# A graph network on one core: the node matrix as one float32r product of 258 columns, with every part of the step in a new order

## The chip, the cores and the metric

The kernel runs on one core of a Trainium2 chip. The metric is the device time of one execution in microseconds (us). The engines are named as in the profile: PE (TensorE, with PEld for its weight loads), DVE (VectorE), ACT (ScalarE), POOL (GpSimd) and SP (SyncE, which issues most transfers here).

## The reference

There are 128 graphs of 128 nodes with 512 features. Each goes through two layers. Cut to what matters:

```python
h = maximum(layernorm(x), 0)
# layer 0
H  = (adj != 0)                       # 128 x 128 of zeros and ones
w  = adj[0, :]                        # first row, a weight for each column
Dn = 1 / (H @ w)                      # per node
Be = 1 / H.sum(axis=0)                # per column
S(v) = Dn * (H @ (Be * (H.T @ v)))
r = layer_norm(relu(S(h @ W1.T) + b1), gamma, beta)     # 1024 wide
x = x + (S(r @ W2.T) + b2 + h)
# layer 1
h = maximum(layernorm(x), 0)
agg = adj @ h / maximum(adj.sum(axis=1), 1e-6)
x = x + relu(concat(h, agg) @ W.T)
```

`H @ diag(Be) @ H.T` is a symmetric 128 x 128 matrix. The kernel calls it the node matrix and computes it once for each graph; `H @ w` is one more column of the same product.

## The kernel before

One graph is worked on as a whole: its 128 nodes lie on the 128 partitions. The large weights stay in SBUF. Each of them, and each activation that meets one, is kept as three float32r parts: high `h`, low `l` and a rest `d`. A product with a weight (`product`) is eight or sixteen 512-column matmuls into one PSUM bank (high with high, low with low) and four or eight with the rests into a second bank. Products are named by their PSUM tiles: `rm`/`rd` for W1 (two halves, with `w10` and `w11`), `gm`/`gd` for W2, `bm`/`bd` and `am`/`ad` for the two halves of W.

Two products are in plain float32, which PE runs as two passes: `conv1_nodes` (`pz`, the node matrix on h, four matmuls of 128 columns) and `node_matrix` (`ps_s`, the node matrix itself, 128 columns and one for `H @ w`).

The program is a software pipeline. `head` starts the first graphs and splits the weights, `step(s)` runs once for s = 3 to 124, and `tail` ends. In a step several graphs are in work: s + 2 (its incidence matrix), s + 1 (node matrix and `conv1_nodes`), s and s - 1 (layer 0), s - 2, s - 3 and s - 4 (layer 1). The calls in `head`, `step` and `tail` are written out by hand, and every engine runs its instructions in exactly that order. Nothing reorders them.

What the change and the prediction touch:

- `load_adjb` brings adj in blocks of 32 x 32. `incidence` transposes it on DVE (L385), scales the column of weights (L387), makes zeros and ones and counts them (L389), bounds the count (L391) and inverts it (L392). `incidence_scale` multiplies by the inverse. `node_matrix` (L404) is the product, and ACT copies it to `s` (L406).
- `node_scale` makes `Dn` from the last column with four small DVE instructions (L415 to L418).
- `conv1_high`, `conv1_low`, `conv1_rest` split `pz` into `z` (ACT L460, DVE L464 and L467). `conv1_weights` multiplies it with W1. `conv1_main` (ACT L509) and `conv1_out` (DVE L514) bring the result back, and `conv1_bias` adds b1 on POOL (L81).
- `inner_sums`, `inner_spread`, `scales`, `shifts`, `inner_norm` are the layer norm. `inner_out` and `inner_in` send its result through DRAM to transpose blocks, `inner_turn` (DVE L550) turns within blocks, and `inner_high`, `inner_low`, `inner_rest` split it.
- `conv2_weights` multiplies with W2, `conv2_weights_out` (DVE L653) brings it back, `conv2_bias` adds on POOL, `conv2_high`, `conv2_low`, `conv2_rest`, `node_high`, `node_rest` (L682, L683) split both sides, and `conv2_nodes` (L701 to L703) multiplies; `conv2_out` (L713) adds the result to x.
- `layer1_*` and `mean_*` are layer 1. `mean_operator` sums adj (L339), bounds and inverts the sum (L340, L341), `mean_scale` scales adj, `mean_out` and `mean_in` send it through DRAM, `aggregate` multiplies, `finish` (L803) adds to x.
- `residual` adds h to x on POOL and then b2: for graphs 3 to 120 by a transfer on POOL's queue that accumulates into x (`moved`, L91), for the other ten by POOL additions.
- `combine` (L81) is the helper of all plain additions and subtractions; on POOL it works in pieces of 256 columns. `scaled` (L301 on ACT, L303 elsewhere) is the helper of all products with a column. `fill` puts products without use ahead of others.

PSUM has six banks for large products and two that `ps_s`, `pz` and `py` share.

Of the kernel before, what the change touches and what calls it, by code (L numbers as in the profile page):

```python
# [7 lines left out]
FP = mybir.dt.float32  # L8
# [8 lines left out]
EPS_DEG = 1e-6  # L17
# [7 lines left out]
def gnn_kernel(  # L25
# [61 lines left out]
    def steady(g):  # L87
        return FIRST <= g <= LAST
# [71 lines left out]
    b2_bc = const.tile([P, D], FP, name="b2_bc")  # L160
    c0 = const.tile([P, D], FP, name="c0")
    gb = const.tile([P, 2, KH], FP, name="gb")
# [169 lines left out]
    SB, HT, S, DN, H0, Z, PZ, SPLIT = ({} for _ in range(8))  # L332

    @stage
    def mean_operator(g):

        a = ADJ.pop(g)
        deg = small.tile([P, 1], FP, tag="deg", name="deg", bufs=2)
        nc.vector.tensor_reduce(deg, a, AX.X, ADD)  # L339
        nc.vector.tensor_scalar(deg, deg, EPS_DEG, 1.0 / 4096.0, MAX, MUL)  # L340
        nc.vector.reciprocal(deg, deg)  # L341
        ADJ[g] = a, deg
# [37 lines left out]
    @stage  # L380
    def incidence(g):


        HT[g] = at = pool.tile([P, P], FP, tag="ht", name="adjt")
        nc.vector.transpose(at, ADJB.pop(g))  # L385
        SB[g] = sb = small.tile([P, P + 1], FP, tag="sb", name="sb")
        nc.vector.tensor_scalar(sb[:, P : P + 1], at[:, 0:1], DOWN_12, None, MUL)  # L387
        cnt = small.tile([P, 1], FP, tag="cnt", name="cnt", bufs=2)
        nc.vector.tensor_scalar(at, at, 0.0, None, ALU.not_equal, ADD, accum_out=cnt)  # L389

        nc.vector.tensor_scalar(cnt, cnt, 1.0, None, MAX)  # L391
        nc.vector.reciprocal(cnt, cnt)  # L392
        SB[g] = sb, cnt

    @stage
    def incidence_scale(g, eng):
        SB[g], cnt = SB[g]
        scaled(eng, SB[g][:, :P], HT[g], cnt)


    @stage
    def node_matrix(g):
        ps = small_bank("ps_s")
        nc.tensor.matmul(ps[:, : P + 1], HT.pop(g), SB.pop(g), start=True, stop=True)  # L404
        s = small.tile([P, P + 1], FP, tag="s", name="s", bufs=4)
        copy(s, ps[:, : P + 1], AF.Copy, scale=4096.0 if steady(g) else 1.0)  # L406
        S[g] = s[:, :P]
        DN[g] = s[:, P : P + 1]

    @stage  # L410
    def node_scale(g):
        w = DN[g]
        DN[g] = dn = small.tile([P, 4], FP, tag="dinv", name="dinv", bufs=6)
        inv = dn[:, 2:3]
        nc.vector.tensor_scalar(inv, w, TINY, None, MAX)  # L415
        nc.vector.reciprocal(inv, inv)
        nc.vector.scalar_tensor_tensor(dn[:, 0:1], w, 0.0, inv, ALU.is_gt, MUL)
        nc.vector.tensor_scalar(dn[:, 1:2], dn[:, 0:1], ONE_UP, None, MUL)  # L418
        if not steady(g):
            nc.vector.tensor_scalar(dn[:, 3:4], dn[:, 0:1], DOWN_12, None, MUL)  # L420
# [14 lines left out]
    @stage  # L435
    def residual(g, eng=nc.gpsimd):
        combine(eng, X[g], X[g], H0[g], ADD)
        if steady(g):
            moved(X[g], b2_bc)
        else:  # L440
            combine(eng, X[g], X[g], b2_bc, ADD)
# [373 lines left out]
    def step(s):  # L815
        node_high(s - 2)
        layer1_high(s - 3)
        conv2_bias(s - 2)
        inner_out(s - 1)
        inner_in(s - 1)  # L820
        conv2_high(s - 2)
        node_rest(s - 2)
        node_matrix(s + 1)
        mean_out(s - 3)
        layer1_low(s - 3, nc.vector)
        layer1_self_main(s - 4)
        conv1_weights(s, 1)
        mean_in(s - 3)
        conv2_low(s - 2, nc.vector)
        layer1_self_out(s - 4)  # L830
        conv2_rest(s - 2)
        conv2_nodes(s - 2)
        finish(s - 4)
        load_adj(s - 2)
        layer1_rest(s - 3)
        x_norm(s + 1)
        conv1_main(s, 0)
        conv2_out(s - 2)
        store(s - 4)
        conv1_nodes(s + 1)  # L840
        conv1_main(s, 1)
        conv1_out(s, 1)
        conv1_out(s, 0)
        conv1_high(s + 1)
        conv1_bias(s, 1)
        layer1_mean(s - 3)
        inner_turn(s - 1)
        layer1_sums(s - 2)
        conv1_bias(s, 0)
        conv1_low(s + 1)  # L850
        layer1_self(s - 3)
        layer1_mean_main(s - 3)
        layer1_spread(s - 2)
        load_adjb(s + 3)
        inner_high(s - 1)
        scales(s - 2, 3)
        mean_transpose(s - 3)
        shifts(s - 2, 3, nc.gpsimd)
        layer1_norm(s - 2)
        inner_sums(s)  # L860
        layer1_mean_out(s - 3)
        layer1_mean_high(s - 3)
        inner_low(s - 1, nc.vector)
        mean_rest(s - 3)
        inner_rest(s - 1)
        layer1_mean_low(s - 3, nc.vector)
        layer1_mean_rest(s - 3)
        inner_spread(s)
        scales(s, 2)
        shifts(s, 2, nc.gpsimd)  # L870
        conv2_weights(s - 1)
        layer1_trip_out(s - 2)
        residual(s + 1)
        incidence(s + 2)
        inner_norm(s)
        aggregate(s - 3)
        node_scale(s + 1)
        load_x(s + 2)
        mean_operator(s - 2)
        conv2_main(s - 1)  # L880
        layer1_trip_in(s - 2)
        conv2_weights_out(s - 1)
        x_sums(s + 2)
        x_spread(s + 2)
        mean_scale(s - 2, nc.scalar)
        conv1_rest(s + 1)
        layer1_turn(s - 2)
        incidence_scale(s + 2, nc.gpsimd)
        conv1_weights(s + 1, 0)
        scales(s + 2, 1)  # L890
        shifts(s + 2, 1, nc.vector)

    def head():
        load_w1(0, 0)
        load_x(0)
        load_adjb(0, nc.scalar)
        copy(eps_root, eps, AF.Sqrt)
        w1[0].high(0)
        w1[0].low(0)
        incidence(0)  # L900
        load_x(1)
        x_sums(0)
        x_sums(1, "A")
        fill(128)
        x_spread(0)
        load_w1(0, 1)
        w1[0].high(1)
        scales(0, 1)
        shifts(0, 1, nc.scalar)
        unit()  # L910
        load_adjb(1)
        incidence_scale(0, nc.vector)
        w1[0].low(1)
        x_norm(0)
        node_matrix(0)
        load_w1(1, 0)
        incidence(1)
        w1[0].rest(0, nc.vector)
        load_w1(1, 1)
        load_w2(0)  # L920
        incidence_scale(1, nc.scalar)
        w1[0].rest(1, nc.vector)
        conv1_nodes(0)
        load_affine()
        load_x(2)
        conv1_high(0)
        x_spread(1)
        conv1_low(0)
        w1[1].high(0)
        fill(128)  # L930
        conv1_rest(0)
        w1[1].high(1)
        load_bias(b2_bc, b2)
        load_bias(b1_bc, b1)
        scales(1, 1)
        node_matrix(1)
        residual(0)
        w1[1].low(0)
        shifts(1, 1, nc.scalar)
        conv1_weights(0, 0)  # L940
        x_norm(1)
        conv1_nodes(1)
        w1[1].low(1)
        load_w2(1)
        beta_row(0)
        beta_row(1)
        w1[1].rest(0, nc.vector)
        conv1_high(1, True)
        scale_w2(1, nc.gpsimd)
        w1[1].rest(1, nc.vector)  # L950
        x_sums(2)
        scale_w2(0, nc.scalar)
        beta_row(2)
        x_spread(2)
        beta_row(3)
        node_scale(0)
        conv1_low(1)
        scales(2, 1)
        scale_w2(2, nc.gpsimd)
        conv1_main(0, 0)  # L960
        scale_w2(3, nc.scalar)
        conv1_weights(0, 1)
        shifts(2, 1, nc.scalar)
        w2[0].high(0)
        conv1_main(0, 1)
        conv1_out(0, 0)
        w2[0].high(1)
        conv1_rest(1)
        conv1_out(0, 1)
        conv1_bias(0, 1, nc.vector)  # L970
        x_norm(2)
        conv1_weights(1, 0)
        load_adjb(2)
        w2[0].low(1)
        incidence(2)
        conv1_bias(0, 0)
        incidence_scale(2, nc.vector)
        beta_row(4)
        inner_sums(0)
        inner_spread(0)  # L980
        beta_row(5)
        beta_row(6)
        residual(2)
        scales(0, 2)
        scale_w2(4, nc.scalar)
        node_scale(1)
        shifts(0, 2, nc.scalar)
        load_adjb(3)
        beta_row(7)
        residual(1)  # L990
        scale_w2(7, nc.vector)
        inner_norm(0)
        beta_out()
        load_w3(1)
        node_matrix(2)
        w2[0].low(0)
        conv1_nodes(2)
        incidence(3)
        scale_w2(5, nc.scalar)
        scale_w2(6, nc.gpsimd)  # L1000
        w2[1].high(0)
        w2[0].rest(1)
        inner_out(0)
        conv1_high(2)
        w2[1].low(0)
        w2[0].rest(0)
        load_x(3)
        conv1_low(2)
        conv1_weights(1, 1)
        conv1_main(1, 0)  # L1010
        incidence_scale(3, nc.scalar)
        conv1_out(1, 0)
        conv1_main(1, 1)
        w2[1].high(1)
        inner_in(0)
        node_matrix(3)
        conv1_rest(2)
        conv1_bias(1, 0)
        conv1_out(1, 1)
        load_w3(0)  # L1020
# [423 lines left out]
```

## Time and profile before

| | us |
|---|---|
| median of 3 runs (2457.92 to 2458.43) | 2458.43 |
| profiled execution | 2458.89 |
| its span | 2457.1 |
| one step of the loop, between two starts of L404 | 18.86 |
| PE busy | 2437.2 |
| DVE busy | 2340.8 |
| ACT busy | 2061.8 |
| POOL busy | 1016.1 |

The span runs from the first to the last profiled instruction, and the time of the execution contains it. Busy times of instructions on one engine overlap a little, since the next may start before the last element of the one before is out. For PE, the distance between two starts is the surer measure.

### The profile page before, as it was taken

What the parts mean: (1) busy time and instruction counts of PE and PEld (TensorE: products, weight loads), DVE (VectorE), ACT (ScalarE), POOL (GpSimd) and SP (SyncE); (2) the same over time, 40 slices, a digit from 0 to 9 for tenths busy, and PEclk for the clock granted to TensorE, in tenths of its full rate; (3) what the DMA queues carried; (4) which work ended last, traced back from release to release, by engine and by line L of the source; (5) the groups of instructions that cost most, each with busy time, mean ns of one, the idle gap of its engine ahead of it and who ended that gap; (6) DMA issues with size and microseconds to landing.
All of it is one profiled execution on the core that took longest, in us unless ns stands there. A gap on an engine that the chain in (4) does not pass through costs nothing.

```text
span 2457.1 us, 41143 instructions
## 1 busy us (share of the span) xinstructions
PE 2437.2 (99%) x11300; PEld 2023.8 (82%) x11300; DVE 2340.8 (95%) x5358; ACT 2061.8 (84%) x4494; POOL 1016.1 (41%) x1560
## 2 busy tenths in 40 slices
PE   8999999999999999999999999999999999999998
PEld 6788888888888888888888888888888888888886
DVE  8899999999999999999999999999999999999987
ACT  8888888888888888888888888888888888888885
POOL 5434343444344434443444434343434343434452
PEclk9999999999999999999999999999999999999999
DMA  7454554445444544454455444544554454445432
GB/s 193 132 139 136 141 143 139 136 142 146 136 137 140 149 135 138 139 150 132 139 144 145 136 138 142 143 136 138 144 141 137 138 146 139 136 138 145 127 121 94
DMA packets 425943, 342.30 MB, mean 139 GB/s; under 512 B 178544, under 2 KB 341872, under 8 KB 425712
## 3 DMA queue, kind: packets, MB, share of 16 engines
q1 hardware_dynamic: 407888, 308.66, 41.0%
q0 software_dynamic: 17248, 30.95, 7.2%
q8 instruction: 89, 1.46, 0.3%
q14 instruction: 142, 1.16, 0.2%
q10 hardware_dynamic: 576, 0.07, 0.0%
HBM read 166.21 MB, written 142.34 MB: 126 GB/s over the span
## 4 chain that ended last, share of the span: by engine, by line
PE 83%; DVE 12%; issue 2%; ACT 2%; DMA 1%; SPq 0%; POOL 0%; DVEq 0%; ACTq 0%; POOLq 0%
PE gm L489 16%; PE rm L489 16%; PE bm L489 8%; PE am L489 8%; PE gd L494 8%; PE rd L494 8%; PE bd L494 4%; PE ad L494 4%; PE pz L447 4%; PE am L791 2%; PE ad L791 1%; DVE r L514 1%; PE ps_s L404 1%; PE yd L703 1%; PE ym L701 1%
## 5 line engine op out<-in xcount | busy, mean ns | idle before, releaser
L81 POOL TENSOR_TENSOR r<-r,b_bc 128x256 f32<-128x256 f32 x500 | 355.5, 743 | 772.5 <-DVE r L514 481.4
L303 POOL TENSOR_SCALAR st<-st 128x1 f32<-128x1 f32 x252 | 76.1, 302 | 566.9 <-DVE st L320 566.9
L460 ACT ACTIVATE z<-pz 128x512 fp32r<-128x512 f32 x128 | 76.5, 598 | 206.3 <-PE pz L447 206.3
L329 ACT ACTIVATE r<-r,st 128x1024 f32<-128x1024 f32 x128 | 159.3, 1244 | 76.7 <-POOL st L303 76.6
L81 POOL TENSOR_TENSOR g<-g,c 128x256 f32<-128x256 f32 x246 | 211.1, 1019 | 3.8 <-DVE g L653 3.8
L329 ACT ACTIVATE h<-x_t,st 128x512 f32<-128x512 f32 x255 | 206.2, 809 | 1.1 <-DVE st L303 0.4
L81 POOL TENSOR_TENSOR x_t<-x_t,h 128x256 f32<-128x256 f32 x256 | 184.7, 742 | 5.8 <-ACT h L329 5.8
L314 ACT ACTIVATE h<-x_t,st 128x512 f32<-128x512 f32 x255 | 183.5, 720 | 4.1
L514 DVE SCALAR_TENSOR_TENSOR r<-rd,dinv,r 128x512 f32<-128x512 f32 x256 | 179.8, 742 | 3.7 <-ACT r L509 1.8
L309 ACT ACTIVATE h<-x_t 128x512 f32<-128x512 f32 x255 | 159.5, 626 | 8.4 <-DVE x_t L713 5.5
L509 ACT ACTIVATE r<-rm,dinv 128x512 f32<-128x512 f32 x256 | 162.2, 690 | 4.2 <-PE rm L489 4.1
L550 DVE STREAM_TRANSPOSE nt<-nb 128x1024 f32<-128x1024 f32 x127 | 156.8, 1235 | 2.5 <-DMA nb<-n_scratch 2.5
L580 DVE SCALAR_TENSOR_TENSOR nd<-nh,nl 128x1024 fp32r<-128x1024 f32 x127 | 154.8, 1219 | 0.0
L81 DVE TENSOR_TENSOR nl<-nt,nh 128x1024 fp32r<-128x1024 f32 x126 | 152.2, 1208 | 0.0
L489 PE MATMUL rm<-w11h,z 128*128 128x512 f32 x512 | 152.0, 418 | 0.0
L489 PE MATMUL bm<-w30h,hh 128*128 128x512 f32 x504 | 146.9, 413 | 0.1
L447 PEld LDWEIGHTS pz<-s,h 128*128 128x128 f32 x1024 | 134.4, 192 | 13.7 <-ACT s L406 1.8
L314 ACT ACTIVATE junk<-r,st 128x1024 bf16<-128x1024 f32 x128 | 145.1, 1134 | 0.1
L489 PE MATMUL rm<-w11l,z 128*128 128x512 f32 x512 | 138.2, 392 | 0.0
L494 PE MATMUL rd<-w11d,z 128*128 128x512 f32 x512 | 138.0, 391 | 0.0
L447 PE MATMUL pz<-s,h 128*128 128x128 f32 x1024 | 135.9, 276 | 1.9 <-ACT s L406 1.3
L489 PE MATMUL rm<-w10h,z 128*128 128x512 f32 x512 | 137.7, 391 | 0.0
(240 smaller groups left out, 7527.0 us busy)
## 6 DMA issues: line engine op xcount, KB each, us to landing
n_scratch<-r SPq DMA_DIRECT2D x128, 512.0 KB, 2.6
nb<-n_scratch SPq DMA_DIRECT2D x508, 128.0 KB, 2.8
x_t<-in_x_dram SPq DMA_DIRECT2D x128, 256.0 KB, 2.8
h_scratch<-h SPq DMA_DIRECT2D x127, 256.0 KB, 2.0
hb<-h_scratch SPq DMA_DIRECT2D x508, 64.0 KB, 2.0
out_dram<-o SPq DMA_DIRECT2D x127, 256.0 KB, 2.1
x_t<-b_bc POOLq DMA_DIRECT2D x118, 256.0 KB, 3.7
adj_t<-in_adj_dram SPq DMA_DIRECT2D x128, 64.0 KB, 2.0
```

The source lines that it names most:

```text
L81: eng.tensor_tensor(dst[:, s], a[:, s], b[:, s], op)
L309: copy(junk, src, func, accum_out=t[:, 0:1])
L314: copy(junk, src, AF.Square, bias=t[:, 1:2], accum_out=t[:, 2:3])
L329: copy(dst, src, func, bias=t[:, 5:6], scale=t[:, 4:5])
L447: nc.tensor.matmul(z[:, k * P : (k + 1) * P], H0[g][:, k * P : (k + 1) * P], S[g], start=True, stop=True)
L460: copy(h, pz, AF.Copy, scale=DOWN)
L489: nc.tensor.matmul(pm, left[i](k), right(i, k), start=(i == 0 and k == 0), stop=(i == 1 and k == kk - 1))
L494: nc.tensor.matmul(pd, left[2](k), right(2, k), start=(k == 0), stop=(k == kk - 1), skip_group_check=True)
L509: copy(R[g][:, HALVES[half]], PY.pop((g, half)), AF.Copy, scale=DN[g][:, 1:2])
L514: nc.vector.scalar_tensor_tensor(r, PR.pop((g, half)), dn[:, 0:1], r, MUL, ADD)
L550: nc.vector.transpose(nt.rearrange("p k (i b) -> p k i b", b=B), t.rearrange("p i k a -> p k i a"))
L580: nc.vector.scalar_tensor_tensor(t, h, 2.0**-12, low, MUL, SUB)
```

## The change

It has four parts.

1. **Node matrix.** The zeros and ones are exact in float32r. The right side (the inverse counts and the weights) is split into a high and a low part of 129 columns each, which stand side by side. One float32r product of 258 columns takes the place of the float32 product of 129. ACT copies the high half to `s` as before, and `node_sum` on DVE adds the low half.
2. **Small work in lines of its own.** The bounds, inverses and scalings that stood inside `incidence`, `node_scale` and `mean_operator` become parts with an engine as argument: `incidence_weight`, `incidence_count`, `incidence_inverse`, `incidence_high`, `node_floor`, `node_up`, `mean_degree`, `mean_inverse`. In the loop `incidence_weight` and `node_floor` are on POOL, the others on DVE. `incidence_scale` has two halves, one on DVE and one on ACT.
3. **b2.** Its rows are copied to a DRAM tile at the start, and the accumulating transfer of `residual` reads them there, for all graphs.
4. **Order.** All calls of `head`, `step` and `tail` stand in a new order, and some change engine. In the loop `layer1_low` goes from DVE to POOL, `mean_scale` from ACT to DVE, and the shift of layer 1 from POOL to ACT. PE's order within a step stays as it was.

```diff
-    b2_bc = const.tile([P, D], FP, name="b2_bc")
+    b2_rows = dram.tile([P, D], FP, tag="b2", name="b2_scratch", bufs=1)
...
     def incidence(g):
-        HT[g] = at = pool.tile([P, P], FP, tag="ht", name="adjt")
-        nc.vector.transpose(at, ADJB.pop(g))
-        SB[g] = sb = small.tile([P, P + 1], FP, tag="sb", name="sb")
-        nc.vector.tensor_scalar(sb[:, P : P + 1], at[:, 0:1], DOWN_12, None, MUL)
-        cnt = small.tile([P, 1], FP, tag="cnt", name="cnt", bufs=2)
-        nc.vector.tensor_scalar(at, at, 0.0, None, ALU.not_equal, ADD, accum_out=cnt)
-        nc.vector.tensor_scalar(cnt, cnt, 1.0, None, MAX)
-        nc.vector.reciprocal(cnt, cnt)
-        SB[g] = sb, cnt
+        raw = pool.tile([P, P], FP, tag="raw", name="raw")
+        nc.vector.transpose(raw, ADJB.pop(g))
+        HT[g] = at = pool.tile([P, P], FP, tag="ht", name="adjt").bitcast(FR)
+        two = small.tile([P, 2], FP, tag="cnt", name="cnt", bufs=2)
+        nc.vector.tensor_scalar(at, raw, 0.0, None, ALU.not_equal, ADD, accum_out=two[:, 1:2])
+        SB[g] = two, raw
...
+    def incidence_high(g):
+        two = SB[g][0]
+        t = small.tile([P, 2 * P + 4], FP, tag="sb", name="sb")
+        SB[g] = sb = t.bitcast(FR)
+        h, l = sb[:, P : 2 * P + 3 : P + 2], sb[:, 2 * P + 1 : 2 * P + 4 : 2]
+        copy(h, two, AF.Copy, scale=DOWN)
+        nc.vector.tensor_tensor(l, two, h, SUB)
+        SPLIT["sb", g] = t[:, 2 * P + 2 : 2 * P + 3], t[:, 2 * P + 3 : 2 * P + 4]
-    def incidence_scale(g, eng):
-        SB[g], cnt = SB[g]
-        scaled(eng, SB[g][:, :P], HT[g], cnt)
+    def incidence_scale(g, i, eng):
+        c = SPLIT["sb", g][i]
+        scaled(eng, SB[g][:, i * (P + 1) : i * (P + 1) + P], HT[g], c)
 
     def node_matrix(g):
-        ps = small_bank("ps_s")
-        nc.tensor.matmul(ps[:, : P + 1], HT.pop(g), SB.pop(g), start=True, stop=True)
+        PS[g] = ps = small_bank("ps_s")
+        nc.tensor.matmul(ps[:, : 2 * P + 2], HT.pop(g), SB.pop(g)[:, : 2 * P + 2], start=True, stop=True)
         s = small.tile([P, P + 1], FP, tag="s", name="s", bufs=4)
         copy(s, ps[:, : P + 1], AF.Copy, scale=4096.0 if steady(g) else 1.0)
+        S[g] = s
+    def node_sum(g):
+        s = S[g]
+        nc.vector.scalar_tensor_tensor(s, PS.pop(g)[:, P + 1 : 2 * P + 2], 4096.0 if steady(g) else 1.0, s, MUL, ADD)
...
     def residual(g, eng=nc.gpsimd):
         combine(eng, X[g], X[g], H0[g], ADD)
-        if steady(g):
-            moved(X[g], b2_bc)
-        else:
-            combine(eng, X[g], X[g], b2_bc, ADD)
+        moved(X[g], b2_rows)
```

The new step, first half:

```python
conv2_bias(s - 2)
node_high(s - 2)
node_rest(s - 2)
inner_out(s - 1)
conv2_high(s - 2)
conv2_low(s - 2, nc.vector)
node_matrix(s + 1)
mean_out(s - 3)
inner_in(s - 1)
layer1_self_main(s - 4)
layer1_high(s - 3)
node_sum(s + 1)
conv1_main(s, 0)
load_adj(s - 2)
conv1_weights(s, 1)
conv2_rest(s - 2)
x_norm(s + 1)
layer1_self_out(s - 4)
conv1_main(s, 1)
layer1_low(s - 3)
conv1_out(s, 0)
conv2_nodes(s - 2)
conv2_out(s - 2)
layer1_rest(s - 3)
mean_in(s - 3)
layer1_sums(s - 2)
conv1_out(s, 1)
conv1_bias(s, 1)
conv1_nodes(s + 1)
inner_turn(s - 1)
mean_operator(s - 2)
layer1_mean(s - 3)
load_adjb(s + 3)
finish(s - 4)
layer1_mean_main(s - 3)
layer1_self(s - 3)
layer1_spread(s - 2)
layer1_mean_out(s - 3)
inner_high(s - 1)
store(s - 4)
scales(s - 2, 3)
conv1_high(s + 1)
shifts(s - 2, 3, nc.scalar)
```

Second half:

```python
layer1_mean_high(s - 3)
conv1_bias(s, 0)
incidence(s + 2)
layer1_norm(s - 2)
load_x(s + 2)
inner_sums(s)
inner_low(s - 1, nc.vector)
mean_transpose(s - 3)
inner_rest(s - 1)
incidence_count(s + 2, nc.vector)
inner_spread(s)
node_floor(s + 1, nc.gpsimd)
layer1_mean_low(s - 3, nc.vector)
layer1_mean_rest(s - 3)
incidence_inverse(s + 2)
scales(s, 2)
mean_degree(s - 2, nc.vector)
incidence_weight(s + 2, nc.gpsimd)
mean_rest(s - 3)
conv2_weights(s - 1)
shifts(s, 2, nc.gpsimd)
conv1_low(s + 1)
conv2_main(s - 1)
incidence_high(s + 2)
conv2_weights_out(s - 1)
incidence_scale(s + 2, 0, nc.vector)
inner_norm(s)
incidence_scale(s + 2, 1, nc.scalar)
mean_inverse(s - 2)
x_sums(s + 2)
layer1_trip_out(s - 2)
aggregate(s - 3)
layer1_trip_in(s - 2)
node_scale(s + 1)
residual(s + 1)
conv1_rest(s + 1)
node_up(s + 1, nc.vector)
layer1_turn(s - 2)
conv1_weights(s + 1, 0)
x_spread(s + 2)
scales(s + 2, 1)
mean_scale(s - 2, nc.vector)
shifts(s + 2, 1, nc.vector)
```

## Prediction, made before the changed kernel was run

> **What bounds the kernel now.** I read the busy shares first, then one step of the PE timeline, then the waits, then the groups with shapes kept apart. The page:
>
> ```profile
> ## 1 busy us (share of the span) xinstructions
> PE 2437.2 (99%) x11300; PEld 2023.8 (82%) x11300; DVE 2340.8 (95%) x5358; ACT 2061.8 (84%) x4494; POOL 1016.1 (41%) x1560
> ...
> PE   8999999999999999999999999999999999999998
> ...
> PEclk9999999999999999999999999999999999999999
> ```
>
> PE is busy in 99% of the span at full clock, DVE in 95%. So PE sets the time, and DVE is near enough to take over. The PE waits, all of them:
>
> ```profile
> PE ps_s L404 <- DVE sb L303: 7.7, 1, 7.7
> PE py L697 <- DVE g L81: 1.7, 2, 1.0
> PE pz L447 <- ACT s L406: 1.3, 2, 0.7
> ...
> PE wd L202 <- DVE g L653: 0.2, 1, 0.2
> ```
>
> They sum to some 15 us and are single events of head and tail: in the 122 steps of the loop PE waits for nobody. One step, from the PE timeline (start, length):
>
> ```profile
> 1197.56 0.38 PE L404 MATMUL ps_s<-sb,adjt 128*128 128x129 f32 x2
> 1197.69 1.18 PE L489 MATMUL rm<-w11h,z 128*128 128x512 f32 x4
> 1198.71 1.08 PE L489 MATMUL rm<-w11l,z 128*128 128x512 f32 x4
> ...
> 1200.55 0.39 PE L701 MATMUL ym<-gp,sp 128*128 128x512 f32 x1
> ...
> 1216.42 0.38 PE L404 MATMUL ps_s<-sb,adjt 128*128 128x129 f32 x2
> ```
>
> A step is 1216.42 - 1197.56 = 18.86 us. Only starts count here, since ends are modelled and overlap: four 512-column float32r products take 0.907 us start to start, 0.227 each. From L404 to L701 there are 2.99 us, of which the twelve rm/rd products need 12 x 0.227 = 2.72. So the float32 node matrix (two passes of 129 columns, and slower starts of the products just behind them) costs **0.27 us a step**.
>
> Ten steps together, and the rows that the steps below use (busy us, mean ns, idle before):
>
> ```profile
> core 0: us, PE busy (x) PEld busy (x) DVE busy (x) ACT busy (x) POOL busy (x), PEclk, DMA share, GB/s
> 1198.00:1386.60 188.60, 188.60 (x881) 157.59 (x880) 182.29 (x421) 159.78 (x351) 77.46 (x120) 1.00 0.49 140
> ```
>
> ```profile
> L682 DVE SCALAR_TENSOR_TENSOR sp<-sp,s 128x128 fp32r<-128x128 f32 x118 | 62.4, 529 | 0.2 <-ACT sp L676 0.2
> L417 DVE SCALAR_TENSOR_TENSOR dinv<-s,dinv 128x1 f32<-128x1 f32 x128 | 48.7, 380 | 4.4
> L683 DVE SCALAR_TENSOR_TENSOR sp<-sp,s 128x128 fp32r<-128x128 f32 x118 | 32.9, 279 | 0.0
> L418 DVE TENSOR_SCALAR dinv<-dinv 128x1 f32<-128x1 f32 x128 | 19.7, 154 | 4.4
> L303 DVE TENSOR_SCALAR sb<-adjt,cnt 128x128 f32<-128x128 f32 x2 | 0.6, 288 | 0.0
> ```
>
> Per step DVE is busy 18.23, ACT 15.98, POOL 7.75 us. L682 and L683 do the same work, and L682 takes 250 ns more. In the timeline it starts at 1215.77, inside POOL's additions on g (1214.39 to 1216.12), and ends just after them; L417 likewise lies under POOL's additions on x_t.
>
> **What the Trainium skill says.** "SBUF — State Buffer", section Who interferes with whom: a VectorE instruction with two SBUF inputs and a GpSimd instruction that reads SBUF exclude each other, and the first one keeps the ports for its whole length. L682 and L417 (+0.25, +0.22 us) agree. "TensorE: Matmul & The Clock Gate", section LDWEIGHTS: a load takes P/1.2 ns, so about 107 ns for 128 columns; the passes of L404 and L447 start 109 to 112 ns apart, which agrees. The same page, Back-to-back issue gap: N/2.4 + 2.5 ns warm for one product alone; the trace's 227 ns at 512 is that (216) plus 11.
>
> **The change, part by part.**
>
> *Node matrix on PE.* Two float32 passes become one float32r product of 258 columns, not in the trace of before. Lower bound: its share of a 512-column product, 258/512 x 227 = 114 ns. Upper bound: a whole slot of 227 plus the 0.04 us of slow starts behind it that L404 shows, 0.27, no gain. I take N/2.4 + 2.5 plus the 11 ns, 121, and half of the slow starts, 0.14 in all, because a weight load (109) fits beside it. Saved: 0.27 - 0.14 = **0.13 us a step** (0 to 0.16). The other 78 float32r products and the eight passes of L447 stay, in the same order. 122 steps x 0.13 = 15.9, and six nodes outside the loop 0.8: **16.7 us**, if no other engine holds PE up.
>
> *DVE.* Start to start, from the timeline. Away: layer1_low (0.60, to POOL), L387 (0.19, to POOL), L415 (0.17, to POOL). New: mean_scale from ACT and the first half of incidence_scale (288 ns long, so 0.21 each, as L389 with 286), node_sum (as L371, 0.20), the low part of two columns (as L387, 0.10 to 0.19). Also the small operations used to follow each other and waited 35 ns each for the one before; L391 and L340 now stand between other work, 0.19 each becoming about 0.08. Sum: -0.96 + 0.77 - 0.22 = **-0.4 us**, to about 17.8 of 18.73. DVE is no bound by its load.
>
> *ACT.* mean_scale (0.39) goes; the other half of incidence_scale (0.39), one shift (0.28) and a two-column copy (0.20) come: 16.5. *POOL.* incidence_scale (0.91) and that shift (0.30) go; layer1_low (two pieces, 1.5), L415 and L387 (0.30 each) come: 8.6. Both have room. ps_s is now given back by node_sum on DVE, at about t = 1.0 of the step, not by ACT; its next user is a step away.
>
> *Bias b2.* The accumulating transfer now reads rows in DRAM, and all 128 nodes use it, not 118. It landed in 3.7 us; conv2_out needs it three steps later. Even at twice that it is hidden. Ten nodes lose their POOL additions (17.2 us in head and tail), beside other work. The queues carry the same 18 transfers a step on SP. There mean_out now stands ahead of the four inner_in and waits for mean_scale at the end of the DVE step: I put inner_in at 0.6 to 2.4 us of the step (before: about 1 us before its start), landing by 5.2, inner_turn at 6.3. One us is left.
>
> *Head and tail.* Counted over the usual distances of starts, PE loses 16 us in the head and 9 in the tail before, the last products' drain among them; the filling products are 768 columns instead of 256 and 512, ahead of work that PE waits for anyway. In the head weight loads now queue behind b2 and three small loads, but incidence(0) no longer stands behind a weight split: PE's first wait (7.7) shortens while the first rm (13.6) does not. I take -2 us for both (+8 to -8).
>
> **Tight places of the step.** I lay the new order along PE's clock, t = 0 at node_matrix.
> 1. From the end of gd (1213.18) to rd (1215.51) are 2.33 us. DVE must do in them conv2_weights_out 0.61, incidence_scale 0.21, two reciprocals 0.10 + 0.20, L417's successor 0.16 (0.42 beside POOL), conv1_rest 0.68: 1.96 to 2.22. Before, three of these were not in between. It just fits; 0.1 us over would cost 12 us.
> 2. conv2_out cannot start before ym, t = 3.5. Then 0.87 + 0.67, layer1_rest 0.62, conv1_out 0.66, inner_turn 1.16, the sum over adj 0.24: finish, with two SBUF inputs, is reached at 7.7. POOL begins its four additions on r at 6.36, 0.71 each, two to 7.8, two to 9.2. Before, no DVE instruction with two SBUF inputs fell into these. Everything hangs on who gets the ports at 7.8.
>
> **Rivals.**
> *A, the forecast:* DVE gets in between the two pairs, finish ends at 8.4, inner_low (1.13) follows mean_out and incidence and ends by 11.5, ahead of its matmul at 11.7. For it: at 2375.79 an addition on DVE that met two POOL pieces took 1.25 us instead of 0.68, so it went between them. 2458.4 - 16.7 - 2 = 2439.7, say **2440**, range 2430 to 2450.
> *B, POOL keeps the ports:* finish waits until 9.2, and behind it in DVE's order mean_out, the transpose of adjb and inner_low, which ends at 12.25. The gm products with w20l start at 11.7 in an unhindered step: PE waits 0.55 us each step. A step is 18.73 + 0.55 = 19.3, 122 x 0.42 = +51: about 2508. It is slower from a wait of 0.13 us on. For it: one L682 met two POOL pieces and took 1.79 us, after both. Against it: the order puts the second pair of additions behind finish, and most meetings in head and tail ended for DVE after one piece.
> *C, the product of 258 columns takes a full slot, or place 1 overruns by 0.1 us:* nothing gained in the loop, 2450 to 2463. Against it: the load price above.
> *D, head and tail lose over 20 us:* little speaks for it, as PE fills 8 tenths of the first slice now.
>
> **How the numbers follow.** A 0.62, B 0.22, C 0.10, D 0.06. The sum is made against the profiled execution, 2458.89 with a span of 2457.1; that is 0.46 above the median 2458.43, so nothing is to be moved. A run of this kernel can tell about 0.2% (4.9 us) from no change. Faster by more than that: A and four tenths of C, 0.66. Within: most of the rest of C and half of D, 0.09. Slower: B and half of D, 0.25. The range runs from 2430 to 2485: it leaves out about 3 in 100 below and the upper half of B and a part of D, some 15 in 100. A's own range is 2430 to 2450.
>
> **What would show it.** Right: node_matrix starts 18.7 us apart in the PE timeline, the rm products start 0.12 to 0.16 us after it, PE waits only in head and tail, DVE busy below 18 us a step. Place 1 wrong: a PE wait on DVE's conv1_rest in each of 122 steps. B: a PE wait on inner_low 122 times, finish over 1 us long beside POOL's r additions. C: the node matrix group at over 0.25 us of start-to-start time. The forecast is wrong if steps are above 18.82 us.

## The result: 2639 us in place of 2458, and one instruction behind it

The changed kernel takes **2639.23 us** (median of 4 runs, 2638.77 to 2639.39), the kernel before 2458.34 in the same comparison. The ratio is 1.0736, with a 95% interval of 1.0717 to 1.0754. The forecast was 2440, and its range ended at 2485.

The page of the kernel after: busy shares, two rows of the slices, the chain, and two groups (busy us, mean ns of one, idle before it).

```profile
PE 2453.9 (93%) x11170; PEld 2001.7 (76%) x11170; DVE 2441.5 (93%) x5489; ACT 2093.8 (79%) x4749; POOL 1430.1 (54%) x1797
...
PE   7999999999999999999999999999999999999998
...
PEclk9999999999999999999999999999999999999999
...
PE 74%; DVE 16%; issue 3%; DMA 3%; ACT 2%; SPq 1%; POOL 1%; DVEq 0%; POOLq 0%; ACTq 0%
PE gm L530 16%; PE rd L535 9%; DVE dinv L457 9%; PE bm L530 8%; PE rm L530 8%; PE am L530 8%; PE gd L535 8%; PE bd L535 4%; PE ad L535 4%; PE pz L488 4%; DVE g L694 3%; DVE sb L303 1%; DMA h_scratch<-h 1%; PE yd L744 1%; PE ym L742 1%
...
L535 PE MATMUL rd<-w10d,z 128*128 128x512 f32 x512 | 151.9, 418 | 154.7 <-DVE dinv L303 130.2
...
L457 DVE SCALAR_TENSOR_TENSOR dinv<-s,dinv 128x1 f32<-128x1 f32 x128 | 233.6, 1825 | 4.4
```

PE's busy time hardly grew. Its share fell from 99% to 93%, at full clock. In the slices this shows nowhere, because a "9" begins at 90%: the loss is spread evenly over the loop. The chain names what fills it: DVE's L457, 9% of the span. That instruction multiplies two columns of *one* element each. It took 380 ns before (as L417) and takes 1825 now. Right behind it PE's `rd` products stand idle for 154.7 us, and before they never did in the loop. The PE waits say whom they waited for (us in total, times, longest):

```profile
PE rd L535 <- DVE dinv L303: 130.2, 98, 1.6
PE rd L535 <- DVE z L508: 24.5, 18, 1.6
PE ps_s L433 <- ACT st L315: 12.9, 1, 12.9
```

116 waits of about 1.3 us, one in nearly each step. The releaser is written as L303 in most, but in DVE's order L303 (`node_up`) stands behind L508 (`conv1_rest`), whose result `rd` needs. It is L508 that comes late. One step in the timelines of PE, DVE and POOL (start, length, in brackets the idle time before):

```profile
1223.34 1.07 PE L530 MATMUL rm<-w10l,z 128*128 128x512 f32 x4
1225.74 1.19 PE L535 MATMUL rd<-w10d,z 128*128 128x512 f32 x4 [1.34 <-DVE dinv L303]
1226.78 0.28 PE L433 MATMUL ps_s<-sb,adjt 128*128 128x258 f32 x1
1226.90 1.08 PE L530 MATMUL rm<-w11h,z 128*128 128x512 f32 x4
```

```profile
1221.95 0.69 DVE L694 SCALAR_TENSOR_TENSOR g<-gd,g 128x512 f32<-128x512 f32 x1 [0.23 <-PE gd L535]
1222.56 0.28 DVE L303 TENSOR_SCALAR sb<-adjt,sb 128x128 fp32r<-128x128 f32 x1
1222.75 0.15 DVE L350 RECIPROCAL deg<-deg 128x1 f32<-128x1 f32 x1
1222.83 0.14 DVE L456 RECIPROCAL dinv<-dinv 128x1 f32<-128x1 f32 x1
1223.01 2.09 DVE L457 SCALAR_TENSOR_TENSOR dinv<-s,dinv 128x1 f32<-128x1 f32 x1
1225.02 0.67 DVE L508 SCALAR_TENSOR_TENSOR z<-z,pz 128x512 fp32r<-128x512 f32 x1
```

```profile
1220.97 1.44 POOL L81 TENSOR_TENSOR x_t<-x_t,h 128x256 f32<-128x256 f32 x2
1222.71 0.90 POOL L91 DMA_DIRECT2D x_t<-b_scratch  x1 [0.30 <-POOL x_t L81]
1223.35 1.72 POOL L81 TENSOR_TENSOR g<-g,c 128x256 f32<-128x256 f32 x2
```

Read the last two together. L457 begins at 1223.01, while POOL issues the accumulating transfer of b2 (`moved`), and ends at 1225.10, when POOL's *two* additions on g are over (1225.07). L508 is queued behind it. It is tight place 1 of the prediction, in every step.

PE's second line shows the other half: from L433 to the next start are 0.12 us. The new product is as cheap as forecast. In four steps of the 120 nothing at this place was held: L457 took 160 ns, and they are 18.70 to 18.73 us long, while the median step has 20.33. In three of the four the issue began only after L457. In the fourth (819 us) issue and additions stood as in the step above; why L457 was let through there stays open.

From the PE timeline: node matrices 5 to 125 are 2436.9 us apart (before 2264.8, so +172.1), the head up to node matrix 5 takes 89.8 (84.2, +5.6), the rest 109.5 (108.1, +1.4). The loss is in the loop.

### The profile page after: what moved, and what is told of

Its sections match the earlier page's. It is cut to its first block, busy times and chain, and to the rows that moved or that the text cites. A ratio compares the mean times of both kernels' runs of the same rounds, so it can differ in the third digit from the quotient of the medians.

```text
span 2636.2 us, 41870 instructions
## 1 busy us (share of the span) xinstructions
PE 2453.9 (93%) x11170; PEld 2001.7 (76%) x11170; DVE 2441.5 (93%) x5489; ACT 2093.8 (79%) x4749; POOL 1430.1 (54%) x1797
## 4 chain that ended last, share of the span: by engine, by line
PE 74%; DVE 16%; issue 3%; DMA 3%; ACT 2%; SPq 1%; POOL 1%; DVEq 0%; POOLq 0%; ACTq 0%
PE gm L530 16%; PE rd L535 9%; DVE dinv L457 9%; PE bm L530 8%; PE rm L530 8%; PE am L530 8%; PE gd L535 8%; PE bd L535 4%; PE ad L535 4%; PE pz L488 4%; DVE g L694 3%; DVE sb L303 1%; DMA h_scratch<-h 1%; PE yd L744 1%; PE ym L742 1%
## 5 line engine op out<-in xcount | busy, mean ns | idle before, releaser
L81 POOL TENSOR_TENSOR r<-r,b_bc 128x256 f32<-128x256 f32 x498 | 408.9, 853 | 414.5 <-DVE r L555 405.0
L81 POOL TENSOR_TENSOR hl<-ht,hh 128x256 fp32r<-128x256 f32 x246 | 178.5, 747 | 411.5 <-ACT hh L612 411.5
L535 PE MATMUL rd<-w10d,z 128*128 128x512 f32 x512 | 151.9, 418 | 154.7 <-DVE dinv L303 130.2
L535 PEld LDWEIGHTS rd<-w10d,z 128*128 128x128 f32 x512 | 87.0, 188 | 216.2 <-DVE z L508 135.4
L457 DVE SCALAR_TENSOR_TENSOR dinv<-s,dinv 128x1 f32<-128x1 f32 x128 | 233.6, 1825 | 4.4
L303 POOL TENSOR_SCALAR st<-st 128x1 f32<-128x1 f32 x131 | 56.8, 434 | 253.2 <-DVE deg L345 236.1
L555 DVE SCALAR_TENSOR_TENSOR r<-rd,dinv,r 128x512 f32<-128x512 f32 x256 | 189.6, 741 | 2.0 <-ACT r L550 1.2
L550 ACT ACTIVATE r<-rm,dinv 128x512 f32<-128x512 f32 x256 | 176.6, 692 | 2.9 <-DMA n_scratch<-r 2.8
L435 ACT ACTIVATE s<-ps_s 128x129 f32<-128x129 f32 x128 | 35.7, 279 | 160.7 <-PE ps_s L433 160.7
L303 POOL TENSOR_SCALAR cnt<-raw 128x1 f32<-128x1 f32 x123 | 152.8, 1243 | 9.8
```

The source lines that it names most:

```text
L81: eng.tensor_tensor(dst[:, s], a[:, s], b[:, s], op)
L303: eng.tensor_scalar(dst, src, c, None, MUL)
L457: nc.vector.scalar_tensor_tensor(dn[:, 0:1], w, 0.0, dn[:, 2:3], ALU.is_gt, MUL)
L535: nc.tensor.matmul(pd, left[2](k), right(2, k), start=(k == 0), stop=(k == kk - 1), skip_group_check=True)
L550: copy(R[g][:, HALVES[half]], PY.pop((g, half)), AF.Copy, scale=DN[g][:, 1:2])
L555: nc.vector.scalar_tensor_tensor(r, PR.pop((g, half)), dn[:, 0:1], r, MUL, ADD)
```

## The experiments

**Theory:** L457 reads two tensors from SBUF, stands in DVE's order where POOL goes over from the transfer to the additions on g, and is held until both are done. **Rivals:** DVE has too much work before `rd` anyway; a value that L457 needs comes late; the issue of the transfer itself holds the ports; the shorter product or the head is at fault. All changes are to the kernel after unless it says otherwise.

### Move the held instruction

```diff
# e1_scale_early, in step
+        node_scale(s + 1)        # behind layer1_mean_rest(s - 3)
...
-        node_scale(s + 1)        # was behind layer1_trip_in(s - 2)
```

> The changed kernel with node_scale(s + 1) alone moved within the step, to just behind layer1_mean_rest(s - 3), where POOL waits for scales(s, 2) and adds nothing. Theory 1 (the 181 us are the wait of node_scale's instruction with two SBUF inputs, L457, for POOL's DMA issue and its two additions on g, which lies between gd and the rd products): L457 falls from 1825 ns to about 160, PE's waits for conv1_rest go, the step falls from 20.33 to the 18.72 us that four lucky steps of the changed kernel show, 122 x 1.61 = 196 us, so about 2443 us and 0.6% faster than before. Rival (DVE as a whole is too slow in the new order, or other places stall once this one goes): the step stays above 19.3, over 2510 us.

2463.64 us, ratio to before 1.0023 (1.0013 to 1.0033). L457 takes 164 ns and the median step is 18.747 us. So moving one reciprocal and one tiny product gives back 175.6 of the 180.9 us. It doesn't become faster than before, and misses its 2443 by 20 us: the mean step is 18.883, 0.136 above the median. Some steps are irregular, and that is taken up below.

### Take away its second tensor

```diff
# e2_one_input
-        nc.vector.scalar_tensor_tensor(dn[:, 0:1], w, 0.0, dn[:, 2:3], ALU.is_gt, MUL)
+        nc.vector.tensor_scalar(dn[:, 0:1], w, 0.0, dn[:, 2:3], ALU.is_gt, MUL)
```

> The changed kernel with L457 in its place, but as a product with a column from SBUF: one tensor input and the inverse as a scalar operand[...]. Theory 1 (ports shared with POOL): about 160 ns and a step of 18.7 us, about 2443 us. Rival (L457 waits for a value, say node_floor on POOL or the sum of s, not for a port): it still takes about 2 us and the time stays at 2639.

2465.85 us, 1.0031 (1.0020 to 1.0042); L457, at its late place, takes 214 ns on average. It needs the same values from the same instructions, but reads one of them as a column scalar. So no late value held it. It was the second tensor input. L508 behind it, with one input from SBUF and one from PSUM, took its usual 0.68 us beside the same two additions.

### Put the urgent work first

```diff
# e3_rest_first, in step
         conv2_weights_out(s - 1)
+        conv1_rest(s + 1)
         incidence_scale(s + 2, 0, nc.vector)
...
-        conv1_rest(s + 1)        # was behind residual(s + 1)
```

> The changed kernel with conv1_rest(s + 1) moved ahead of the half of incidence_scale, the two reciprocals and L457, just behind conv2_weights_out(s - 1). The wait of L457 stays (1.5 to 2 us), but PE's rd products no longer stand behind it. If the wait costs time only because conv1_rest is queued behind it: a step of 18.7 to 18.9 us, 2443 to 2465 us. If 2 us more on DVE are too many whatever is behind them (my sum of DVE is 17.4 plus 1.5 to 2.0): a step of 19.0 to 19.5 us, 2477 to 2540 us.

2594.96 us, 1.0554 (1.0538 to 1.0569), above both forecasts. L457 is free here (194 ns on average), and yet the kernel takes 136 us more than before. DVE's timeline shows who took its place:

```profile
1142.46 0.68 DVE L508 SCALAR_TENSOR_TENSOR z<-z,pz 128x512 fp32r<-128x512 f32 x1
1143.06 2.08 DVE L303 TENSOR_SCALAR sb<-adjt,sb 128x128 fp32r<-128x128 f32 x1
...
1145.31 0.16 DVE L457 SCALAR_TENSOR_TENSOR dinv<-s,dinv 128x1 f32<-128x1 f32 x1
```

`incidence_scale`, a product of one tensor with a column, is held for the same 2.08 us. `rd` has its input in time, but DVE has lost 2 us of a step in which it has little over: it is busy in 96% of the span, and PE's weight loads wait at `yd` and `bd` instead (72.8 and 58.5 us in all). The Trainium skill offers a reason, in "SBUF — State Buffer", Who interferes with whom: a `tensor_scalar` can run in a mode that uses both port pairs, and then contends with GpSimd as well. The 2.08 us agree with it, though the trace doesn't show in which mode L303 ran; L457 of e2, which is one element wide, was not held (0.21 us).

### Take away POOL's additions, or the transfer

```diff
# e4_bias_dve, in step
-        conv2_bias(s - 2)
+        conv2_bias(s - 2, nc.vector)
```

> The changed kernel with conv2_bias(s - 2) on DVE in the loop, so POOL's two additions on g are gone, while the issue of the b2 transfer stays at its place (16.27 to 17.17 us of the step, L457 arrives at 16.57). If the additions on g hold the ports: L457 160 ns, step 18.7 plus what 0.6 us more on DVE may cost, 2443 to 2470 us. If the DMA issue on POOL holds them too: L457 about 0.6 us, ending with the issue, and a PE wait of 0.1 to 0.3 us a step, 2455 to 2480 us.

2497.87 us, 1.0160 (1.0144 to 1.0175), above both forecasts. L457 is free. POOL's and DVE's timelines:

```profile
1141.19 0.90 POOL L91 DMA_DIRECT2D x_t<-b_scratch  x1 [0.30 <-POOL x_t L81]
```

```profile
1141.49 0.16 DVE L457 SCALAR_TENSOR_TENSOR dinv<-s,dinv 128x1 f32<-128x1 f32 x1
```

L457 runs through in the middle of the issue, so **the issue alone holds nobody**. The same section of the skill infers this, since generating descriptors needs the write side only; here it is 0.16 us. The step (median 19.03) is still long, most likely because DVE has the addition as well; that was not tried by itself.

```diff
# e5_no_b2: residual without moved(X[g], b2_rows)
# e11_issue_last, in the loop
         conv2_bias(s - 2)
+        if 4 <= s <= N - 4:
+            moved(X[s], b2_rows)      # no longer in residual
```

> This kernel leaves the addition of b2 out (no accumulating transfer at all, so POOL has nothing between its two additions on x_t and its two on g). If the additions alone hold the ports, L457 must still wait for both: POOL starts them right behind conv2_weights_out (L694), at about 0.6 us before L457 is due, so L457 takes 1.0 to 1.4 us in place of 2.09, PE's wait per step drops by about 0.8 to a step of 19.2 to 19.6 us, 2510 to 2560 us in all. If the issue of the accumulating transfer is part of what holds DVE up, L457 takes 0.16, a step is 18.72 and the time is about 2460. If DVE gets in between the two additions, L457 takes 0.5 us and the step is about 18.8.

> The kernel after with the accumulating transfer of b2 issued by POOL behind its two additions on g instead of between the additions on x_t and those on g; all work is still done, and node_scale stays in its late place. In e5_no_b2, without that transfer, L457 took 0.53 us: it got in after the first of the two additions. If it was the issue just ahead that let both additions run as one block in the kernel after, L457 takes 0.5 to 0.6 us here too, the step is 18.79 and the time 2456 to 2475 us. If it was the transfer's traffic, or anything else that e5 left out with it, L457 takes some 2 us again and the time is about 2639.

e5 takes 2457.77 us, 0.9998 (0.9990 to 1.0007), e11 2462.75, 1.0017 (1.0010 to 1.0024). Nothing but POOL's order differs between e11 and the kernel after, for graphs 4 to 124; `node_scale` stands at its late place, and the additions are all there. DVE and POOL of e11:

```profile
1142.27 0.53 DVE L457 SCALAR_TENSOR_TENSOR dinv<-s,dinv 128x1 f32<-128x1 f32 x1
1142.72 0.67 DVE L509 SCALAR_TENSOR_TENSOR z<-z,pz 128x512 fp32r<-128x512 f32 x1
```

```profile
1140.23 1.43 POOL L81 TENSOR_TENSOR x_t<-x_t,h 128x256 f32<-128x256 f32 x2
1142.04 1.44 POOL L81 TENSOR_TENSOR g<-g,c 128x256 f32<-128x256 f32 x2 [0.37 <-POOL x_t L81]
1143.43 0.87 POOL L91 DMA_DIRECT2D x_t<-b_scratch  x1
```

L457 begins inside the first addition and ends with it, at 1142.80: it is let in between the two. So neither additions nor transfer suffice to hold it for both. At graph 125 the same execution keeps the old order, with the issue ahead, and there L457 is held as in the kernel after:

```profile
2366.40 2.07 DVE L457 SCALAR_TENSOR_TENSOR dinv<-s,dinv 128x1 f32<-128x1 f32 x1
```

```profile
2366.09 0.90 POOL L91 DMA_DIRECT2D x_t<-b_scratch  x1 [0.30 <-POOL x_t L81]
2366.74 1.71 POOL L81 TENSOR_TENSOR g<-g,c 128x256 f32<-128x256 f32 x2
```

An issue ahead is not enough either. In one step of the kernel after, DVE had g ready only at 1041.68, late in the issue; in the step shown above it was ready before the issue began. POOL's additions had to wait for it, and L457 got in after the first:

```profile
1042.04 0.56 DVE L457 SCALAR_TENSOR_TENSOR dinv<-s,dinv 128x1 f32<-128x1 f32 x1
```

```profile
1040.89 0.90 POOL L91 DMA_DIRECT2D x_t<-b_scratch  x1 [0.30 <-POOL x_t L81]
1041.77 1.48 POOL L81 TENSOR_TENSOR g<-g,c 128x256 f32<-128x256 f32 x2
```

So what holds L457 for both is **a pair of additions that stand ready behind an issue while it still runs**. The groups of POOL's additions show it too, first in the kernel after, then in e11 (mean ns behind the comma):

```profile
L81 POOL TENSOR_TENSOR g<-g,c 128x256 f32<-128x256 f32 x246 | 210.2, 1023 | 0.8 <-DVE g L694 0.8
```

```profile
L81 POOL TENSOR_TENSOR g<-g,c 128x256 f32<-128x256 f32 x246 | 177.2, 741 | 45.3 <-POOL x_t L81 42.3 <-DVE g L695 1.5 <-issue 1.1
```

Both pairs start 0.70 us apart. Behind the issue each is recorded 1.02 us long, so they overlap by 0.32; in e11 0.74, an overlap of 0.04. This goes with the hold in every case that the traces of the kernel after, e5, e9 and e11 have of L457 (L417 in e9) waiting at this pair: held to the end of the second addition 225 times, with an overlap of 0.31 or more, and let in after the first 241 times, with 0.10 or less. When DVE comes doesn't decide it: twice in the kernel after L457 began 0.14 and 0.20 us after the first addition and was still held for both (1.60 and 1.53 us). That the overlap is how the pair keeps the ports is my reading; it was not tried by itself. The skill's page gives the ports to the first comer for one instruction. Here they stayed with POOL for two, and by the records POOL had them before the recorded start of its first addition (1223.35), since L457 would have needed only until 1223.17.

### The same in the kernel before

```diff
# e9_before_moved: the kernel before, in step
         conv2_weights_out(s - 1)
+        node_scale(s + 1)
...
-        node_scale(s + 1)        # was behind aggregate(s - 3)
```

> The kernel before with one line moved: node_scale(s+1) directly behind conv2_weights_out(s-1), as in the kernel after, POOL's order as it is. If the place of L417 next to POOL's pair of additions on g is the whole cause, L417 (0.38 before) is held there too, for 1 to 2 us, conv1_rest is late behind it, PE waits on it in each step, and the time is 2500 to 2640. If the cause needs the new order of POOL or the shorter product, the time stays within 5 us of 2458. As POOL has the half of a us of its column product in this order, a hold of less than 0.4 us would also hide.

2651.04 us, 1.0783 (1.0767 to 1.0799), a little above its forecast: **the whole loss, from one moved line**, without anything else of the change. Its group, one step and its waits:

```profile
L417 DVE SCALAR_TENSOR_TENSOR dinv<-s,dinv 128x1 f32<-128x1 f32 x128 | 217.0, 1696 | 4.3
```

```profile
1228.49 1.90 DVE L417 SCALAR_TENSOR_TENSOR dinv<-s,dinv 128x1 f32<-128x1 f32 x1
```

```profile
1227.42 0.90 POOL L91 DMA_DIRECT2D x_t<-b_bc  x1 [0.30 <-POOL x_t L81]
1228.08 0.91 POOL L303 TENSOR_SCALAR sb<-adjt,cnt 128x128 f32<-128x128 f32 x1
1228.66 1.70 POOL L81 TENSOR_TENSOR g<-g,c 128x256 f32<-128x256 f32 x2
```

```profile
PEld rd L494 <- DVE z L467: 208.0, 118, 2.3
...
PE rd L494 <- DVE z L467: 158.9, 113, 1.9
```

In this order a product with a column stands between the issue and the pair, and L417 is held all the same. So the issue need not be right ahead: product and additions each begin before the one ahead has ended. For five late graphs of the kernel before, where POOL adds b2 itself and issues nothing, the same product and pair overlap by no more than 0.07 us.

### The product, the irregular steps, the head

```diff
# e6_float32: e1 with the node matrix of before
-        nc.tensor.matmul(ps[:, : 2 * P + 2], HT.pop(g), SB.pop(g)[:, : 2 * P + 2], ...)
+        nc.tensor.matmul(ps[:, : P + 1], HT.pop(g).bitcast(FP), SB.pop(g)[:, : P + 1].bitcast(FP), ...)
...
-        nc.vector.scalar_tensor_tensor(s, PS.pop(g)[:, P + 1 : 2 * P + 2], 4096.0 if steady(g) else 1.0, s, MUL, ADD)
+        nc.vector.scalar_tensor_tensor(s, PS.pop(g)[:, : P + 1], 0.0, s, MUL, ADD)
```

> The kernel with node_scale moved early (e1_scale_early, 2463.6 us, median step 18.747), with the node matrix as the float32 product of 129 columns again. It leaves out the low part of the column factors: node_sum adds nothing, but runs as before. This prices the part of the change that PE sees. By my sum the float32r product saves 0.13 us a step: a median step of 18.87 to 18.89 and 2478 to 2482 us. If the saving comes from elsewhere (the order of the other engines' work), the step stays at 18.75 and the time at 2464.

2472.32 us, median step 18.860 against 18.747: the float32r product is worth **0.113 us a step** (forecast 0.13). In time e6 is 8.7 us above e1, less than 122 x 0.113 = 13.8, as more of its steps are regular (mean 18.945).

```diff
# e8_trip_early: e1, in step (three calls moved up, none added)
+        scales(s - 2, 3)                  # ahead of layer1_mean_out(s - 3)
...
+        shifts(s - 2, 3, nc.scalar)       # ahead of conv1_high(s + 1)
+        layer1_norm(s - 2)
```

> The kernel with node_scale moved early (e1_scale_early), in which in addition scales(s-2,3) stands ahead of layer1_mean_out on DVE and its shift and layer1_norm(s-2) stand ahead of conv1_high and layer1_mean_high on ACT. layer1_norm then starts at about 9.2 us of the step instead of 10.1, and the transfers of h leave 0.9 us earlier, about where the kernel before has them. If the late h transfers cause the irregular steps (some 16 us in all), most of these go: a mean step of 18.77 to 18.80, 2450 to 2455 us. If they have another cause, the time stays at 2460 to 2467.

2453.93 us, 0.9980 (0.9972 to 0.9988); the mean step is 18.777. The tile view of `h_scratch`, the transfer that carries h to DRAM, says who waited for it (us, times) and how long it took to land, first in e1, then in e8:

```profile
  DVE ht L591: 16.1, 21
  ACT g L690: 10.8, 12
...
DMA to landing us min/median/max: 1.8/2.0/4.5
```

```profile
  DVE ht L591: 3.4, 7
  ACT g L690: 0.5, 1
...
DMA to landing us min/median/max: 1.7/2.0/4.4
```

The view counts the transfer to DRAM (256 KB) and the four that fetch it back (64 KB each) together. The transfers are no quicker: those to DRAM alone land in up to 4.5 us in e1 and 4.4 in e8. In the kernel before they land within 3.2 us, those that fetch back within 3.8, and DVE waited 1.1 us in all. The new order had put `layer1_norm` on ACT so late (10.1 us after the node matrix, before 9.3) that such a landing reached DVE.

The slow landings have a companion in the traces. Of the transfers of h to DRAM that took over 3 us, 12 of 14 in e1 and 8 of 9 in e8 ran beside a 16 KB fetch on an instruction queue; of the quicker ones 4 of 113 and 7 of 118 did. No run changed these fetches, so that they slow the transfers isn't shown by experiment.

```diff
# e10_head: e8, in head (calls moved up, none added)
+        load_x(0), load_adjb(0, nc.scalar), load_w1(0, 0)     # ahead of these two:
         load_bias(b2_rows, b2)
         load_adjb(1)
+        copy(eps_root, eps, AF.Sqrt)                          # ahead of x_sums(0)
...
-        fill(768)
+        fill(128)
# e12_before_head: e8 with the head of the kernel before, the new small
# stages beside those that they come from
# e13_both: e10 with the transfer of b2 behind conv2_bias, as in e11
```

> The kernel e8_trip_early (2453.9 us) with another start: x(0), adjb(0) and the first weights are loaded ahead of b2 and adjb(1), the square root of eps comes ahead of x's sums on ACT, and the filling product ahead of the first rm has 128 columns instead of 768. In e8 the first x landed at 7.3 us and the fillers end 1.2 us after z is ready. If the order of loads is what delays the head, node 5 starts at 85 to 87 us instead of 89.2 and the time is 2449 to 2452. If later waits of the head (weight parts, node 2) set its end, it starts within 1 us of 89.2 and the time is 2453 to 2455.

> The kernel e8_trip_early with the head of the kernel before, its order kept, the new small stages put beside the stages that they come from. The kernel before reaches node 5 at 84.2 us, e8 at 89.2. If the new order of the head is what costs those 5 us, node 5 starts at 83.5 to 85.5 and the time is 2448 to 2450 us. If the new stages (three float32r columns, node_sum, the transfer of b2) cost it, node 5 stays at 87 to 90 and the time is 2452 to 2455.

> The kernel e10_head (2451.5 us) with the transfer of b2 issued behind POOL's additions on g, as in e11_issue_last. In e10 PE waits for nobody in a regular step of 18.747 us, and eight irregular steps cost 4 us. If POOL's additions on g, which now end 0.3 us earlier, give the step some slack that it can use, irregular steps go and the time is 2447 to 2450. If not, it is the same within 2 us.

e10: **2451.53 us**, 0.9971 (0.9960 to 0.9981), and node matrix 5 starts at 87.3. The loads, the square root and the fillers are worth 2 of the 5 us. e12: 2461.39, node matrix 5 at 94.9, worse than either head and outside both forecasts. PE's first waits there:

```profile
PE ps_s L433 <- ACT sb L301: 8.8, 1, 8.8
PE pz L488 <- DVE s L441: 7.0, 2, 5.4
```

Before, `ps_s` waited 7.7 and `pz` 1.3 us. These two waits have grown by 6.8 of the 10.7 us by which node matrix 5 is later (94.9 against 84.2). That fits the longer way to the first node matrix (high part on ACT, low part on DVE, then `node_sum` behind DVE's weight split), but no run took it apart; it looks as if the head of the change, with 12.9 and 2.7 for the same two waits, hides a part of it. e13: 2450.82, 0.9967 (0.9955 to 0.9979), not to be told from e10. Both beat the kernel before by some 7 us. The page of e10, busy shares and chain:

```profile
PE 2423.3 (99%) x11168; PEld 2009.6 (82%) x11168; DVE 2267.7 (93%) x5489; ACT 2095.7 (86%) x4748; POOL 1429.9 (58%) x1797
...
PE 90%; POOL 3%; DVE 2%; ACT 2%; issue 2%; DMA 1%; SPq 0%; ACTq 0%; POOLq 0%; DVEq 0%
```

PE is at 99% again, on a shorter step.

## Why the prediction was wrong, step by step

- **Tight place 1 is the step that failed.** The mechanism and its sign were named (a PE wait on `conv1_rest` in each step), and so was the tariff: 0.1 us over costs 12. The term "L417's successor 0.16 (0.42 beside POOL)" was mis-sized. It measured 2.01 us from start to start, so the place needs 3.79 us from L694 to `rd` where the sum had at most 2.22 of 2.33. What failed is the assumption that one addition at most is waited for; the runs show that both are. The mean step is 20.31 us in place of 18.73, which makes 193 us in 122 steps. Head and tail came out 9 us above the forecast. With the 2440 that is 2642; 2639 was measured.
- **Where the 0.42 came from.** It was an average of L417 in its old place, beside the additions on x_t, which have no issue in front of them. The new place lies beside the additions on g, which do. The trace of before had the pattern: its additions on g, too, have an issue ahead (and the product between) and are recorded 1019 ns long on average, those on x_t 742. L682 met the pair on g, and of two long ones at this place one took 1.21 and one 1.79 us, "after both". The instruction that "went between" two pieces at 2375.79 stood beside additions without an issue ahead. The prediction had both observations, and used them for place 2 only, where the additions have no issue ahead and, as in e11, let DVE in. That some DVE instructions came after one piece and others after both should have been followed up: what stands ahead of the pair on POOL?
- **Tight place 2 was right, as forecast A had it.** `finish` began at 7.6 us of the step, took 0.83 us in place of 0.68 and ended between the two pairs at 8.4 (forecast 7.7 and 8.4); PE waited for nothing there. Rival B had the right mechanism (POOL keeps its ports over two additions) at the wrong place.
- **The node matrix** was right within 0.02 us: 0.113 a step in e6. Rival C's full slot is out.
- **DVE's load** was right: 17.6 us a step in e10 (ten steps: 176.02), forecast 17.8. ACT has 16.3 (16.5). POOL has 11.4 where 8.6 was forecast: its additions on r wait once for DVE, and the two tiny operations L449 and L303 take 1.07 and 1.25 us beside DVE's long subtractions, where 0.30 each was put. PE waits for neither, so no cost shows.
- **b2's transfer** was hidden, as said: it landed in 4.4 us (forecast 3.7). What was missed is that its *issue* sits in front of the two additions. It was so before as well, and the prediction has no term for it. `inner_in` behind `mean_out` was right too: DVE stood idle ahead of `inner_turn` for 1.6 us in the whole kernel after, and for 4.3 in e10.
- **Head and tail** were put at -2 us and measured +7.0 (5.6 and 1.4), inside the bounds of +8 to -8. The first node matrix waits 12.9 us instead of 7.7.
- **The irregular steps** were in no term. With place 1 repaired they cost e1 16 us. The moved `layer1_norm` was checked only against its consumers on a normal step, not against a late landing.

## What to carry to other kernels

When an instruction moves on one engine, look at what the engine that shares its ports does at the new place, and take the price from an instruction that met just that, not from the mean at the old place. Two GpSimd additions that stand ready behind a transfer's issue can hold a VectorE instruction for both; put the issue behind them, as e11 did, or give VectorE there only what has one of its two inputs in PSUM or reads one small tensor, as in e2. Where VectorE works in order, the held instruction's own use is beside the point: ask what is queued behind it.

## What the runs showed of the hardware that I had not expected

- A one-element VectorE product with two SBUF inputs took 2.09 us beside two GpSimd additions, 0.70 us each from start to start, that stood ready behind a DMA issue. The same beside the same additions without the issue ahead took 0.53, 0.56 where the additions became ready only late in the issue, and 0.16 beside an issue with no additions behind.
- A product of a 128 x 128 tensor with a column, one tensor input, was held just as long (2.08 us).
- Single 256 KB transfers of h to DRAM landed after 3.0 to 4.5 us where the median is 2.0 to 2.4, in the kernel before (3.2 at most), e1 and e8. 25 of these 28 ran beside a 16 KB fetch on an instruction queue, and 19 of the 353 quicker ones. From e1 to e8, where they leave 0.9 us earlier, DVE's wait behind them fell from 16.1 to 3.4 us.
